# A four-layer vision block with a selective scan: the inputs of GpSimd's products moved to different 8-byte halves, and one more product in eight on GpSimd

## The chip, the core and the metric

The kernel runs on one core of a Trainium2 chip. The metric is the device time of one execution in microseconds (us). Before the change it is 22073.93 us, the median of three runs (22069.05 to 22075.93). The profile is of one such execution; its span from the first to the last instruction is 22054.7 us.

A core has engines that run at the same time, each with its own instruction queue, which it works through in order. TensorE (PE in the profile) multiplies matrices into PSUM, VectorE (DVE) and ScalarE (ACT) do elementwise work, GpSimd (POOL) does elementwise work [...], and SyncE (SP) issues most of the DMAs. They wait for each other through semaphores.

## What is computed

The input is 8 images of 56 x 56 positions with 192 channels, in float32. Four layers follow each other, each with a normalization ahead of it and a residual sum behind it: a gated layer with Toeplitz products, window attention, a 3 x 3 depthwise convolution, and a selective state-space layer. Only the last one is touched. Cut to what matters:

```python
def _selective_scan(u, delta, A, Bm, Cm, Dp, delta_bias):
    delta = jax.nn.softplus(delta + delta_bias[None, :, :, None])
    dA = jnp.exp(delta[:, :, :, None, :] * A[None, :, :, :, None])
    dBu = (delta * u)[:, :, :, None, :] * Bm[:, :, None, :, :]

    def comb(e1, e2):
        a1, b1 = e1
        a2, b2 = e2
        return (a1 * a2, a2 * b1 + b2)
    _, hs = jax.lax.associative_scan(comb, (dA, dBu), axis=-1)
    y = jnp.einsum('bkdnl,bknl->bkdl', hs, Cm)
    return y + Dp[None, :, :, None] * u
```

Per image there are 384 channels, 16 states per channel, 4 scan directions and 3136 positions. For each of them the state is h[t] = dA[t] * h[t-1] + dBu[t], and the output is the sum of h * C over the 16 states. Behind the scan come a layer normalization, a gate and a projection.

## The kernel before, in words

**Tiles of the scan.** An image's scan is cut into 28 chunks: 4 directions (`slot`) by 7 pieces of CH = 448 positions. Slots 0 and 2 run forward, slots 1 and 3 backward. The 384 channels are ND = 3 blocks of 128 partitions (`d`), the 16 states are NP = 8 groups of NG = 2 (`k`). One (chunk, d, k) is a *pair*: 2 states x 448 positions = 896 elements on 128 partitions. A chunk is 24 pairs, an image 672, the whole kernel 5376.

**What a pair does**, in the order of its steps (line numbers are those of the profile):

- `inject` (L1000, GpSimd): `ring[slot] = du * bm`, 896 elements. `du` is delta times x, 448 elements, read twice (once per state); `bm` is a row of B that a DMA has spread over the partitions. `ring` has 6 slots of 2 x 449 elements. Of the 449, one holds the state carried over from the chunk before (`initial`, L1007, ScalarE), at the front for a forward scan and at the back for a backward one.
- `decay` (L1017, ScalarE): two exponentials of delta, 449 elements each, into PSUM (`ps_a`, two buffers).
- `scan` (L1026, VectorE): one scan over 898 elements, from `ps_a` and the ring slot.
- `times_c` (L1032): `hc = h * cm`, 896 elements. `on_pool` (L995) says which engine takes it: GpSimd for k = 1, 4 and 6, else VectorE. [...]for its pairs the scan writes its result back into the ring slot; for VectorE's pairs it goes to `ps_a`. `hc` has four buffers.
- `keep_state` (L1039, ScalarE): the last state of the chunk is copied out of wherever the scan has put it.
- `add_up` (L1047, TensorE): two matmuls with the identity add the two states into `ps_y`. In float32 each is done in two passes, so the profile counts four. This frees the `hc` buffer.

Three times per chunk GpSimd also makes a `du` (`times_x`, L988, 448 elements, from `delta` and `xcd`).

**Where the tiles begin.** Each tile begins on a multiple of 32 bytes. A ring slot is 2 x 449 x 4 = 3592 bytes, which is 8 more than a multiple of 16, so even slots begin in the lower 8-byte half [...] and odd slots in the upper one; inside a slot, a forward pair begins 4 bytes on and its second state 1796 bytes behind the first. `delta2`, of which one buffer serves even chunks and the other odd ones, has rows of 450 x 4 = 1800 bytes, again 8 more than a multiple of 16, and its data begin 4 bytes into the row. `bm`, `cm`, `xcd` and `du` begin on a multiple of 16.

**The order of the work.** The order of all instructions is fixed when the program is built. The loop over pairs at L1197 writes out, for pair g: `inject(g+2)`, `times_c(g-1)` if it is GpSimd's, `keep_state(g-1)`, `decay(g+1)`, the scan of g, `times_c(g)` if it is VectorE's, the loads of B and C of the next chunk (`load_bc`, on SP's queue), then other work, then `add_up(g-2)`.

The other work comes from a planner (`Parts`, L1062). While image b is scanned, all earlier layers of image b+1 (`front`, L890: `gate`, `attention`, `conv2`, `inner`, `steps`) are put between the pairs in small pieces, and so is the end of image b's own output (`finish`, L897; layer normalization, gate and projection for one piece of 448 positions). The planner keeps a clock for each of four engines (P for GpSimd, A for ScalarE, D for VectorE, E for TensorE) and adds to it the cost in us that the code states for each step: 2.09 for an inject, 2.0 for a GpSimd `times_c`, 1.08 for a `du`, 2.02 for a scan, 1.09 for a VectorE `times_c`, 1.1 for `add_up`; the pieces of other work cost what `Meter` works out from their size. A piece is placed at pair g when its engines' clocks stay under limits that depend on the next scan (L1250); a piece that was refused gets 3 us of grace for each refusal. If something of image b+1 isn't ready when its scan needs it (L1205), the planner places the rest at once, with no pair between.

`finish` has two GpSimd products of 672 elements (L927, L934) on pieces that are carved one behind the other out of one tile, `slab_f`.

Image 0's earlier layers, and the first layer's products for all images, run ahead of the first scan. Image 7's scan has no next image beside it.

Of the kernel before, what the change touches and what calls it, by code (L numbers as in the profile page):

```python
# [15 lines left out]
F32 = mybir.dt.float32  # L16
# [11 lines left out]
CH = 448  # L28
# [6 lines left out]
TC = 24  # L35
NG = 2
NP = NS // NG
SLAB, SLAB_F = 10048, 2688


class Meter:
# [41 lines left out]
def model(ctx: ExitStack, tc: tile.TileContext, a: dict, out: bass.AP):  # L83
# [211 lines left out]
    with (  # L295
# [600 lines left out]

        def finish(b, j):  # L897

            yc, sq, rs, x3 = carve(slab_f, 128, (ND, CH), (ND, CH // 2), (CH // 2,), (2, CH // 2))
            x3 = x3[:CP]  # L900
            n = CH // 2

            def mean(p, src, n):
                for d in range(ND):
                    nc.tensor.matmul(p[:, :n], ones, src[:, d, :], start=d == 0, stop=d == ND - 1)  # L905

            y = ysum[:, :, j * CH : (j + 1) * CH]
            yield 0, 1
            p = bank()
            mean(p, y, CH)  # L910
            yield 1, 0
            nc.vector.tensor_sub(yc, y, p[:, :CH].unsqueeze(1).to_broadcast([128, ND, CH]))  # L912
            for u in range(2):
                yield 0, 0
                tok = slice(j * CH + u * n, j * CH + (u + 1) * n)
                yu = yc[:, :, u * n : (u + 1) * n]
                nc.scalar.activation(sq, yu, AF.Square)  # L917
                yield 0, 1
                p = bank()
                mean(p, sq, n)  # L920
                yield 1, 0
                nc.scalar.activation(rs, p[:, :n], AF.Ln, bias=eps5)  # L922
                nc.scalar.activation(rs, rs, AF.Exp, scale=-0.5)  # L923
                nc.sync.dma_start(out=sq, in_=z_d[b][:, :, tok])
                nc.sync.dma_start(out=x3, in_=blocks(x3_d[b])[:, :, tok])
                yield 0, 0
                nc.gpsimd.tensor_mul(yu, yu, rs.unsqueeze(1).to_broadcast([128, ND, n]))  # L927
                yield 0, 0
                for d in range(ND):
                    nc.scalar.activation(  # L930
                        yu[:, d, :], yu[:, d, :], AF.Identity, scale=ln_g[:, d : d + 1], bias=ln_b[:, d : d + 1]
                    )
                yield 0, 0
                nc.gpsimd.tensor_mul(yu, yu, sq)  # L934
                yield 0, 1
                p = bank()
                for m in range(2):
                    for d in range(ND):
                        nc.tensor.matmul(  # L939
                            p[:CP, m * n : (m + 1) * n],  # L940
                            w_out[:, d, m * CP : (m + 1) * CP],
                            yu[:, d, :],
                            start=d == 0,
                            stop=d == ND - 1,
                        )
                    yield 1, 0
                nc.vector.tensor_add(x3, x3, p[:CP, :CH].rearrange("p (m n) -> p m n", m=2))
                nc.sync.dma_start(out=blocks(out[b])[:, :, tok], in_=x3)
            yield 0, 0
# [34 lines left out]
            nc.sync.dma_start(out=delta[:, :, 1 : CH + 1], in_=dl_d[slot][b][:, :, j * CH : (j + 1) * CH])  # L984

        def times_x(i, d):
            du = dus[i, d] = sp.tile([128, 1, CH], F32, name="du", bufs=3)
            nc.gpsimd.tensor_mul(du[:, 0, :], deltas[i][:, d, 1 : CH + 1], xcs.pop((i, d)))  # L988

        def tokens(i):  # L990

            return (slice(0, CH), CH, 0) if chunks[i][1] % 2 else (slice(1, CH + 1), 0, CH)

        def on_pool(d, k):
            return k in (1, 4, 6)  # L995

        def inject(g):
            i, d, k = pairs[g]
            hs = hss[g] = ring[:, g % 6]
            nc.gpsimd.tensor_mul(hs[:, :, tokens(i)[0]], dus[i, d].to_broadcast([128, NG, CH]), bms[i, k])  # L1000

        def initial(g):

            i, d, k = pairs[g]
            at = NG * (NP * d + k)
            src = zero6 if i % NCH == 0 else states[i - 1].rearrange("p d n -> p (d n)")[:, at : at + 3 * NG]
            nc.scalar.copy(ring[:, g % 6 : g % 6 + 3, :, tokens(i)[1]], src.rearrange("p (q n) -> p q n", n=NG))  # L1007

        def decay(g):
            i, d, k = pairs[g]  # L1010
# [143 lines left out]
        sp = own.enter_context(tc.tile_pool(name="sc", bufs=2))  # L1154
        bcp = own.enter_context(tc.tile_pool(name="bc", bufs=NP))
        ysum = wp2.tile([128, ND, L], F32, name="ysum")
        ring = wp2.tile([128, 6, NG, CH + 1], F32, name="ring")
        delta2 = wp2.tile([128, 2, ND, CH + 2], F32, name="delta2")

        for u in range(2):  # L1160
            nc.gpsimd.memset(delta2[:, u, :, 0 : CH + 2 : CH + 1], 1e30)
# [3 lines left out]
        with tc.manual_schedule():  # L1165
# [11 lines left out]

            def feed(g):
                inject(g)
                fed[g] = run("P", 2.09, taken[g - 6] if g > 5 else 0.0)  # L1180

            def take(g):
                times_c(g)
                after = scanned[g], summed[g - 4] if g > 3 else 0.0
                taken[g] = run("P", 2.0, *after) if on_pool(*pairs[g][1:]) else run("D", 1.09, *after)

            def prepare(g):
                decay(g)
# [8 lines left out]
            for g, (i, d, k) in enumerate(pairs):  # L1197
# [13 lines left out]
                    xcs[i + 1, 2] = load_xc(i + 1, 2)  # L1211
                if more and (d, k) in ((1, 6), (1, 7), (2, 6)):
                    times_x(i + 1, k - 6 if d == 1 else 2)
                    run("P", 1.08)
                pi, pd, pk = pairs[g - 1]
                if g + ahead <= last:
                    feed(g + ahead)
# [145 lines left out]
```

## Time and profile before

| | |
|---|---|
| median of 3 runs | 22073.93 us |
| span of the profiled execution | 22054.7 us |
| PE busy | 18328.2 us (83%) |
| DVE busy | 16637.5 us (75%) |
| ACT busy | 12126.1 us (55%) |
| POOL busy | 16068.5 us (73%) |
| GpSimd's inject, L1000 | 5376 times, 2092 ns each |
| GpSimd's times_c, L1032 | 2016 times, 1958 ns each |
| GpSimd's du, L988 | 672 times, 1058 ns each |
| VectorE's times_c, L1032 | 3360 times, 1092 ns each |
| VectorE's scan, L1026 | 5376 times, 2.02 us each |
| PE, add_up, L1047 | 21504 passes, 591 ns each |

For the profiled execution the span is the only time of its own that is at hand; it is 19.2 us (0.1%) under the median of the runs.

Read such a table with care: a share of busy time is a mean over stages that have different limits. The first scan begins at 3441 us, image 7's at 19999 us. Between these two an image takes 2347 to 2393 us; image 7's scan, with no other image's work beside it, takes 2067 us to the end of the program. A group's mean can also hide several kinds of instruction: the 1958 ns of GpSimd's times_c is a mean over instructions that differ, as the prediction shows. Durations overlap a little on GpSimd: of two instructions that follow each other without a gap the second is reported to start before the first has ended.

### The profile page before, as it was taken

What the parts mean: (1) busy time and instruction counts of PE and PEld (TensorE: products, weight loads), DVE (VectorE), ACT (ScalarE), POOL (GpSimd) and SP (SyncE); (2) the same over time, 40 slices, a digit from 0 to 9 for tenths busy, and PEclk for the clock granted to TensorE, in tenths of its full rate; (3) what the DMA queues carried; (4) which work ended last, traced back from release to release, by engine and by line L of the source; (5) the groups of instructions that cost most, each with busy time, mean ns of one, the idle gap of its engine ahead of it and who ended that gap; (6) DMA issues with size and microseconds to landing.
All of it is one profiled execution on the core that took longest, in us unless ns stands there. A gap on an engine that the chain in (4) does not pass through costs nothing. (4 is left out here: it accounts for less than half of the span.)

```text
span 22054.7 us, 196675 instructions
## 1 busy us (share of the span) xinstructions
PE 18328.2 (83%) x58396; PEld 9752.3 (44%) x58396; DVE 16637.5 (75%) x13276; ACT 12126.1 (55%) x28153; POOL 16068.5 (73%) x8503
## 2 busy tenths in 40 slices
PE   7878977788887889888988888788988898887667
PEld 4845654334443444344443444344444444343333
DVE  2122117997799779987899789977998789977998
ACT  3125114655666465656665576656565666556554
POOL 0000007987889778987888788878898789878999
PEclk9588868999999989999999999898999999998888
DMA  3832575344644465345644464345534564445433
GB/s 88 239 99 49 177 186 165 122 130 162 185 138 125 145 194 152 121 129 180 185 124 128 159 196 137 123 147 189 159 117 131 176 186 125 126 151 184 129 127 110
DMA packets 2419588, 3249.95 MB, mean 147 GB/s; under 512 B 917598, under 2 KB 2361024, under 8 KB 2387554
## 3 DMA queue, kind: packets, MB, share of 16 engines
q1 hardware_dynamic: 2398292, 3121.12, 46.8%
q0 software_dynamic: 15520, 116.14, 1.4%
q8 instruction: 463, 7.59, 0.1%
q14 instruction: 609, 4.99, 0.1%
q10 hardware_dynamic: 4704, 0.12, 0.0%
HBM read 2661.35 MB, written 575.48 MB: 147 GB/s over the span
## 5 line engine op out<-in xcount | busy, mean ns | idle before, releaser
L1000 POOL TENSOR_TENSOR ring<-du,bm 128x896 f32<-128x896 f32 x5376 | 11104.3, 2092 | 17.3 <-DMA bm<-bc 10.1
L1047 PE MATMUL ps_y<-hc,ident_sb 128*128 128x448 f32 x21504 | 9809.0, 591 | 688.5 <-POOL hc L1032 620.9
L1026 DVE TENSOR_TENSOR_SCAN ps_a<-ps_a,ring 128x898 f32<-128x898 f32 x3360 | 6795.9, 2023 | 756.3 <-ACT ps_a L1017 295.2
L1017 ACT ACTIVATE ps_a<-delta,A_logs_sb 128x449 f32<-128x449 f32 x10752 | 6860.2, 638 | 327.8 <-DVE ring L1026 45.5
L1047 PEld LDWEIGHTS ps_y<-hc,ident_sb 128*128 128x128 f32 x21504 | 4281.7, 207 | 4745.4 <-issue 3574.5
L1032 POOL TENSOR_TENSOR hc<-ring,cm 128x896 f32<-128x896 f32 x2016 | 3947.5, 1958 | 2086.0 <-DVE ring L1026 991.9
L1032 DVE TENSOR_TENSOR hc<-ps_a,cm 128x896 f32<-128x896 f32 x3360 | 3668.4, 1092 | 1166.5 <-PE ps_y L1047 880.1
L1026 DVE TENSOR_TENSOR_SCAN ring<-ps_a,ring 128x898 f32<-128x898 f32 x2016 | 4063.3, 2016 | 276.6 <-ACT state L1039 121.0
L1039 ACT COPY state<-ps_a 128x2 f32<-128x2 f32 x3359 | 529.9, 158 | 4120.2 <-DVE hc L1032 4111.2
L278 DVE COPY tzx<-ps_tz 112x448 f32<-112x448 f32 x432 | 269.9, 625 | 1421.9 <-PE ps_tz L272 1289.2
L286 POOL DMA_DIRECT2D o<-tzx x192 | 97.4, 514 | 1686.4 <-DVE tzx L278 1552.5
L272 PE MATMUL ps_tz<-tzx,tm 112*112 112x112 f32 x4608 | 1031.7, 404 | 287.2 <-DMA tm<-ext 272.9
L272 PEld LDWEIGHTS ps_tz<-tzx,tm 112*112 112x112 f32 x4608 | 1028.1, 319 | 326.6 <-issue 320.5
L815 PE MATMUL ps_f<-slab 128*128 128x448 f32 x2646 | 1092.8, 549 | 55.3 <-DMA slab<-dg_d 48.1
L645 PE MATMUL ps_f<-ident_sb,slab 98*98 98x98 f32 x1344 | 335.8, 315 | 558.1 <-ACT slab L638 558.1
L747 PE MATMUL ps_f<-slab 96*96 96x448 f32 x1764 | 729.8, 549 | 42.5 <-DVE slab L734 42.5
L815 PEld LDWEIGHTS ps_f<-slab 128*128 128x128 f32 x2646 | 508.5, 193 | 555.8 <-issue 502.2
L77 PE MATMUL ps_f<-slab 96*96 96x448 f32 (+6 forms) x2306 | 737.8, 501 | 9.3 <-DMA slab<-x 4.1
L988 POOL TENSOR_TENSOR du<-delta,xcd 128x448 f32<-128x448 f32 x672 | 711.0, 1058 | 22.2 <-DMA slab<-in_x_dram 22.2
L1039 ACT COPY state<-ring 128x2 f32<-128x2 f32 x2016 | 378.7, 188 | 609.7 <-DVE ring L1026 581.0
L630 ACT ACTIVATE slab<-slab,mxs 98x98 f32<-98x98 f32 x1344 | 487.6, 364 | 357.8 <-DVE mxs L627 357.8
L482 PE MATMUL ps_f<-ident_sb,slab 112*96 112x112 f32 x4704 | 531.1, 267 | 138.3 <-DVE slab L490 95.0
(218 smaller groups left out, 16966.9 us busy)
## 6 DMA issues: line engine op xcount, KB each, us to landing
bm<-bc SPq DMA_DIRECT2D x1792, 448.0 KB
cm<-bc SPq DMA_DIRECT2D x1792, 448.0 KB
xcd<-xc SPq DMA_DIRECT2D x840, 224.0 KB
dl<-slab SPq DMA_DIRECT2D x224, 672.0 KB
delta<-dl SPq DMA_DIRECT2D x224, 672.0 KB
tzx<-qv SPq DMA_DIRECT2D x192, 588.0 KB
o<-tzx POOLq DMA_DIRECT2D x192, 588.0 KB, 14.2
slab<-x SPq DMA_DIRECT2D x224, 336.0 KB
```

What stands on the lines that cost most here:

```text
L77: return f(*args, **kw)
L272: nc.tensor.matmul(po[:, c, :], t[:, :, c2 + c], x[:, :, c1 + c2 + c], start=True, stop=True)
L482: nc.tensor.matmul(p[:CP, t * TT : (t + 1) * TT], ot[:, n % 2, i, t, c % 2 * CP : c % 2 * CP + CP], ident[:TT, :TT], start=i == 0, stop=i ...
L747: nc.tensor.matmul(p[:CP, :CH], dg[:, k, t, :], xp[:, u, k, dy : dy + 8, dx : dx + W], start=t == 0, stop=t == 8,)
L815: nc.tensor.matmul(p[:, :CH], dg[:, t, :], xp[:, 8 * j + dy : 8 * j + dy + 8, dx : dx + W], start=t == 0, stop=t == 8,)
L988: nc.gpsimd.tensor_mul(du[:, 0, :], deltas[i][:, d, 1 : CH + 1], xcs.pop((i, d)))
L1000: nc.gpsimd.tensor_mul(hs[:, :, tokens(i)[0]], dus[i, d].to_broadcast([128, NG, CH]), bms[i, k])
L1017: nc.scalar.activation(dA[:, n, :], deltas[i][:, d, at : at + CH + 1], AF.Exp, scale=negA[:, slot, d, c : c + 1])
L1026: nc.vector.tensor_tensor_scan(h, dA, hs, 0.0, ALU.mult, ALU.add)
L1032: (nc.gpsimd if on_pool(d, k) else nc.vector).tensor_mul(hc, h[:, :, tokens(i)[0]], cms[i, k])
L1039: nc.scalar.copy(states[i][:, d, NG * k : NG * k + NG], h[:, :, tokens(i)[2]])
L1047: nc.tensor.matmul(yps[i, d][:, :CH], ident, hcs[g][:, n, :], start=k + n == 0, stop=k + n == NP + NG - 2)
```

## The change

It has three parts.

1. **Where inputs begin.** Two elements (8 bytes, `HALF`) are put ahead of the data of `du`, `delta2` and, in `slab_f`, of the piece `sq` and what follows it. A ring slot becomes 900 elements (3600 bytes, a multiple of 16), and the 2 x 449 elements begin 1 element into it for a forward pair and 2 for a backward one, so that the positions themselves (without the carried state) begin 8 bytes [...] in either direction, and those of the second state 12 bytes. The other input (`bm`, `cm`, `xcd`, or the earlier piece of `slab_f`) begins at 0. So the two inputs of every GpSimd product begin in different 8-byte halves.
2. **Who multiplies by C.** `on_pool` gives GpSimd k = 0, 2, 4, 6 in place of k = 1, 4, 6: 12 of a chunk's 24 products in place of 9, or 2688 of 5376 in place of 2016.
3. **What the planner believes.** GpSimd's costs become 1.78 for an inject (2.09), 1.78 for a `times_c` (2.0) and 0.93 for a `du` (1.08).

```diff
-SLAB, SLAB_F = 10048, 2688
+HALF = 2
+SLAB, SLAB_F = 10048, 2688 + HALF
+SLOT = NG * (CH + 1) + HALF
...
-            yc, sq, rs, x3 = carve(slab_f, 128, (ND, CH), (ND, CH // 2), (CH // 2,), (2, CH // 2))
+            yc, _, sq, rs, x3 = carve(slab_f, 128, (ND, CH), (HALF,), (ND, CH // 2), (CH // 2,), (2, CH // 2))
...
-            du = dus[i, d] = sp.tile([128, 1, CH], F32, name="du", bufs=3)
+            du = dus[i, d] = sp.tile([128, 1, HALF + CH], F32, name="du", bufs=3)[:, :, HALF:]
...
         def on_pool(d, k):
-            return k in (1, 4, 6)
+            return k % 2 == 0
+
+        def in_ring(g, n):
+
+            at = 1 + chunks[pairs[g][0]][1] % 2
+            return ring[:, g % 6 : g % 6 + n, at : at + NG * (CH + 1)].rearrange("p q (n t) -> p q n t", n=NG)
 
         def inject(g):
             i, d, k = pairs[g]
-            hs = hss[g] = ring[:, g % 6]
+            hs = hss[g] = in_ring(g, 1)[:, 0]
...
-            nc.scalar.copy(ring[:, g % 6 : g % 6 + 3, :, tokens(i)[1]], src.rearrange("p (q n) -> p q n", n=NG))
+            nc.scalar.copy(in_ring(g, 3)[:, :, :, tokens(i)[1]], src.rearrange("p (q n) -> p q n", n=NG))
...
-        ring = wp2.tile([128, 6, NG, CH + 1], F32, name="ring")
-        delta2 = wp2.tile([128, 2, ND, CH + 2], F32, name="delta2")
+        ring = wp2.tile([128, 6, SLOT], F32, name="ring")
+        delta2 = wp2.tile([128, 2, ND, CH + 2 + HALF], F32, name="delta2")[:, :, :, HALF:]
...
-                fed[g] = run("P", 2.09, taken[g - 6] if g > 5 else 0.0)
+                fed[g] = run("P", 1.78, taken[g - 6] if g > 5 else 0.0)
...
-                taken[g] = run("P", 2.0, *after) if on_pool(*pairs[g][1:]) else run("D", 1.09, *after)
+                taken[g] = run("P", 1.78, *after) if on_pool(*pairs[g][1:]) else run("D", 1.09, *after)
...
-                    run("P", 1.08)
+                    run("P", 0.93)
```

## The prediction

> **What bounds the kernel now.** First the busy shares in 40 slices of the span (551 us each):
>
> ```profile
> PE   7878977788887889888988888788988898887667
> DVE  2122117997799779987899789977998789977998
> POOL 0000007987889778987888788878898789878999
> ```
>
> The scan runs from slice 7 on. No engine is full all the time: PE and DVE change places, and only in the last slices, where PE falls to 6, does POOL stand at 9. So I cut one middle image (scan from 10529 to 12877 us) by what the other work beside it is, and took the busy time of each stretch: gate, attention, conv2, inner, steps; the sixth row is a stretch of image 7, with nothing beside it.
>
> ```profile
> core 0: us, PE busy (x) PEld busy (x) DVE busy (x) ACT busy (x) POOL busy (x), PEclk, DMA share, GB/s
> 10659.00:11096.00 437.00, 409.94 (x1571) 226.80 (x1570) 404.30 (x310) 249.46 (x508) 379.36 (x199) 0.96 0.58 165
> 11096.00:11964.00 868.00, 681.30 (x2371) 333.91 (x2371) 817.18 (x691) 574.84 (x1673) 786.14 (x407) 0.92 0.41 125
> 11964.00:12145.00 181.00, 172.20 (x454) 79.00 (x453) 162.41 (x131) 71.91 (x167) 137.99 (x72) 0.98 0.41 124
> 12145.00:12703.00 558.00, 475.62 (x1293) 245.25 (x1293) 399.52 (x264) 309.41 (x629) 436.70 (x230) 0.92 0.51 165
> 12703.00:12991.00 288.00, 252.20 (x680) 116.00 (x676) 221.65 (x148) 240.12 (x429) 245.17 (x129) 0.92 0.62 209
> 20213.00:21551.00 1338.00, 914.33 (x1864) 403.12 (x1864) 1263.34 (x814) 680.80 (x1553) 1335.74 (x697) 0.87 0.40 130
> ```
>
> Gate and conv2 are TensorE's (94 and 95% busy), attention is VectorE's (94%; PE 78%), inner and steps are TensorE's in bursts (85 and 88%), and image 7 is GpSimd's (99.8%). TensorE's timeline in inner shows a burst: 4 passes of add_up, 6 of the convolution, and again, with no gap.
>
> ```profile
> 12242.36 1.67 PE L1047 MATMUL ps_y<-hc,ident_sb 128*128 128x448 f32 x4
> 12243.87 2.42 PE L815 MATMUL ps_f<-slab 128*128 128x448 f32 x6
> 12246.12 1.67 PE L1047 MATMUL ps_y<-hc,ident_sb 128*128 128x448 f32 x4
> ```
>
> From 12242.36 to 12246.12 is 3.76 us for a pair, where VectorE's own work per pair is 2.70 (2.02 + 5/8 x 1.09). There neither faster products nor fewer VectorE products help.
>
> **Does the half matter?** The kernel before answers it itself, since its ring slots begin in either half. GpSimd's timeline in a backward chunk of image 7:
>
> ```profile
> 20800.25 6.17 POOL L1000 TENSOR_TENSOR ring<-du,bm 128x896 f32<-128x896 f32 x3
> 20806.38 1.77 POOL L1032 TENSOR_TENSOR hc<-ring,cm 128x896 f32<-128x896 f32 x1
> 20808.11 6.17 POOL L1000 TENSOR_TENSOR ring<-du,bm 128x896 f32<-128x896 f32 x3
> 20814.24 2.07 POOL L1032 TENSOR_TENSOR hc<-ring,cm 128x896 f32<-128x896 f32 x1
> 20816.27 4.11 POOL L1000 TENSOR_TENSOR ring<-du,bm 128x896 f32<-128x896 f32 x2
> 20820.35 2.07 POOL L1032 TENSOR_TENSOR hc<-ring,cm 128x896 f32<-128x896 f32 x1
> 20822.38 6.17 POOL L1000 TENSOR_TENSOR ring<-du,bm 128x896 f32<-128x896 f32 x3
> 20828.50 1.78 POOL L1032 TENSOR_TENSOR hc<-ring,cm 128x896 f32<-128x896 f32 x1
> ```
>
> The counts between (3, 2, 3) tell that the products are k = 1, 4, 6, 1. k = 1 lies in an odd slot: both its states begin in the upper half (8 and 12 bytes), `cm` in the lower: 1.77 us. k = 4 and 6 lie in even slots (0 and 4 bytes), the half of `cm`: 2.07. Sorted over the whole trace, the 2016 products have means of 1777 ns (odd, backward), 2085 (even, backward), and 1935 and 1930 for forward ones, whose two states begin in different halves, so that one is with `cm` and one not. `du` splits likewise, by the row of `delta2`: 983 against 1133 ns. So in different halves 896 elements cost 0.31 us less, 448 elements 0.15. All injects, whose inputs both begin at 0, take 2087 ns (median), slot and direction make 4 ns at most: where the output begins doesn't matter.
>
> [...] In the trace the slope is (2085 - 1133) / 448 = 2.13 ns per element for one half, [...] but (1777 - 983) / 448 = 1.77 ns [...] for different halves[...]. [...] here an inject reported as 2.09 takes 2.04 of the queue (6.13 for three), a fast product 1.73, a slow one 2.03, a `du` 1.08 or 0.93. I use these.
>
> **The change, part by part.**
>
> *GpSimd per chunk.* Before: 24 injects x 2.04 + 9 products x 1.91 (mean of 1.73, 2.03 and 1.88 by their frequency) + 3 du x 1.0 = 69.2 us. Image 7 confirms it: 1338 us for 465 pairs (19.4 chunks) is 69.1. After: 24 x 1.73 + 12 x 1.73 + 3 x 0.93 = 65.1, or 4.1 less although three products are added. That an inject drops to 1.73 isn't in the trace (it reads `du` twice); bounds: 1.73, and 2.04 for no effect. I take 1.73, since at the same half it costs what a product costs (2087 against 2085), and `finish`'s two products, one with a repeated input, agree too (1613 and 1610 ns). Those save 0.23 us each, by the same slope; nobody waits there but in the last image.
>
> *VectorE per chunk.* 24 x 2.02 + 15 x 1.09 = 64.8 becomes 61.6: 3.3 less. Scans cost the same whichever tile they write (2016 and 2023 ns).
>
> *What moves.* k = 0 and 2 go to GpSimd, k = 1 goes to VectorE. A GpSimd product is issued one pair later, behind inject(g+2); the C load of the next chunk on SP's queue waits for it, so one load more per chunk is released up to 3 us later, ahead of a use a chunk away. keep_state reads the ring (188 ns, not 158): 20 us over the kernel on ScalarE, which has 40% free. add_up waits for GpSimd in 4 pairs of 8. In the last image TensorE already idles for it (415 us of 1338) at no cost; elsewhere four `hc` buffers cover it.
>
> *By stage, per image* (pairs per stage counted from the scans):
> - Attention, 272 pairs = 11.3 chunks, VectorE-bound: 11.3 x 3.3 = 37 us. GpSimd falls along (786 to about 740), so VectorE stays the bound.
> - Gate, 131 pairs: VectorE would give 18, but PE's 410 of 437 stays; 7 from the bubbles.
> - conv2, 48 pairs, PE and VectorE both near full: 3.
> - Inner, 142 pairs: bursts give nothing; between them pairs run at about GpSimd's 437/142 = 3.1 us and gain 0.15; with some 80 such pairs, 12.
> - Steps, 72 pairs, ScalarE and PE: 3.
>
> Sum 62, for 7 images 434. Image 7: 25 of its 28 chunks are GpSimd-bound, 25 x 4.1 = 103, with `finish` 105. VectorE follows at 61.6 to 65.1, no closer than before (64.8 to 69.2). What ran before 3441 us keeps its time. Total 539.
>
> *The planner.* Its pair gets shorter too, so it has less room per pair for the next image's layers. They begin later from image to image already: `steps` starts at pair 600 of 672 in the first scan, at 657 in the seventh, where the last chunk takes 127 us in place of some 90, since scans wait. A few pairs more per image will make that happen in several images; I take 50 us off: 489. Span 22054.7 - 489 = 21566, and with the 19 us by which the median exceeds the span, **21585 us**; this case's own range is 21450 to 21720. Chance 0.66.
>
> **Rivals.**
> - *The next image's layers fall behind.* If they stretch with the planner's pair (VectorE's 2.70 to 2.565, or 5%: some 30 pairs), they are late from the second image on. One late end costs 38 us (127 against 89), which was an overrun of about 10 pairs; 30 pairs cost about 68 us of bare TensorE work (2.26 each) plus waits, of which part comes back where TensorE is relieved: 45 net, five times: 225. 21810. For: the drift. Against: pieces mostly go one per pair, whatever the pair's length. 0.17.
> - *TensorE's stages gain as well*, because it waits less for products: a third of its idle 154 us per image outside attention, 26 more than I counted, 7 times, and no late ends: 21355. Against: it waited there for DMA, ScalarE and VectorE's small steps. 0.12.
> - *Slower: the repeated `du` hides the half.* Then the inject stays at 2.04, and GpSimd's chunk is 49.0 + 20.8 + 2.8 = 72.6, 3.4 more: image 7 loses 95, attention becomes GpSimd-bound and gains nothing, inner loses some 5 per image: 22190. It decides from an inject of 1.90 on, where the chunk is back at 69.2. 0.05.
>
> **Range and chances.** 21380 to 21850 leaves out the slower rival, the lower half of the gain in TensorE's stages and the worst of the late ends, about 2 in 10. A measurement here can tell 0.2% (44 us) from no change. Faster by more: 0.92; within: 0.03; slower: 0.05.
>
> **What would show it.** Injects and products all at 1.77 to 1.79 us, `du` at 0.98; 2688 products each; image 7's chunks at 65 to 66 us with GpSimd still near 100%; attention at about 830 us with VectorE near 94%; gate and conv2 almost unchanged. An inject above 1.9, chunks beyond 120 us at the ends of images 1 to 5, or attention with both VectorE and GpSimd under 90% would prove me wrong.

## The result, and the profile after

The change takes the median from 22074.93 us (4 runs, 22069.05 to 22098.8) to **21828.74 us** (4 runs, 21800.17 to 21848.46): 246 us less, a ratio of 0.9884 (95% interval 0.987 to 0.9898). The profiled execution spans 21798.4 us, 256 less than before. That is inside the range, and half of the 489 us that I had forecast.

The busy shares of the kernel after, in 40 slices (545 us each), for the three engines that were shown of before:

```profile
PE   7978977888888989888888889888988888887777
DVE  2122117996799768986799769976898589976998
POOL 0000006887789778977788768976898678877998
```

The last slices still read PE 7, POOL 9, DVE 9: image 7 remains GpSimd's. Next, groups of the page after: line, engine, operation, tiles and count, then busy time and mean ns of one, then the engine's idle time ahead of the group and what ended most of it.

```profile
L1007 POOL TENSOR_TENSOR ring<-du,bm 128x896 f32<-128x896 f32 x5376 | 9447.8, 1771 | 1983.9 <-ACT ring L1014 1937.8
L1039 POOL TENSOR_TENSOR hc<-ring,cm 128x896 f32<-128x896 f32 x2688 | 4758.0, 1770 | 860.9 <-DVE ring L1033 349.3
L1039 DVE TENSOR_TENSOR hc<-ps_a,cm 128x896 f32<-128x896 f32 x2688 | 2935.0, 1092 | 974.5 <-PE ps_y L1054 753.3
L990 POOL TENSOR_TENSOR du<-delta,xcd 128x448 f32<-128x448 f32 x672 | 658.6, 980 | 23.6 <-DMA xcd<-xc 23.6
```

The durations are what the change is meant to give: inject 1771 ns (2092 before), GpSimd's `times_c` 1770 (1958), `du` 980 (1058), 2688 products each. The surprise stands at the end of the first line: inject waited **1938 us** for ScalarE's L1014. That is `initial`, the copy of the carried states into the ring (L1007 before). Before, inject waited 17 us in all.

The same stages as in the prediction, for the same image (gate, attention, conv2, inner, steps; the sixth row is a stretch of image 7), as busy time of each engine in each stretch after the change:

```profile
core 0: us, PE busy (x) PEld busy (x) DVE busy (x) ACT busy (x) POOL busy (x), PEclk, DMA share, GB/s
10634.00:11064.00 430.00, 405.99 (x1578) 224.17 (x1576) 389.73 (x296) 249.86 (x512) 360.09 (x215) 0.98 0.58 160
11064.00:11892.00 828.00, 683.53 (x2375) 334.67 (x2375) 780.43 (x658) 575.06 (x1676) 742.01 (x445) 0.89 0.43 131
11892.00:12077.00 185.00, 175.62 (x458) 80.75 (x457) 156.45 (x128) 73.53 (x172) 133.51 (x80) 0.97 0.41 127
12077.00:12660.00 583.00, 488.09 (x1343) 259.36 (x1341) 355.22 (x233) 305.13 (x614) 386.04 (x235) 0.92 0.48 154
12660.00:12991.00 331.00, 274.24 (x666) 118.91 (x666) 233.75 (x150) 252.09 (x448) 248.29 (x150) 0.83 0.63 209
20030.00:21262.00 1232.00, 887.37 (x1790) 382.08 (x1790) 1149.26 (x723) 653.94 (x1489) 1205.41 (x722) 0.87 0.42 138
```

Attention went from 868 to 828 us with VectorE at 94% in both. Inner became longer, 583 against 558, although VectorE and GpSimd have less to do in it (355 against 400 us, 386 against 437). Image 7's GpSimd is at 97.8% where it was at 99.8%.

Two things about these rows have to be known. The stretches, here, in the prediction and for e12 below, were counted from the profiler's own zero, which lies 11.3 us ahead of the first instruction, while the view counts from that instruction; so each begins and ends 11 us after its stage. The same holds for the scan starts given ahead (3441 and 19999 us are 3430 and 19988 on the clock of the views; 10529 and 12877 are 10518 and 12866). Both kernels are shifted alike, and no busy share above moves by more than about three points. And the prediction's row for steps stops 36 us before the next gate begins: the stage took 324 us there, so its 288 must not be compared with the 331 here.

Taken over all images from the traces (each stage from the first matmul of its main work to that of the next; mean of 7 images, of 6 for steps), in us; these durations don't depend on where the clock starts:

| kernel | gate | attention | conv2 | inner | steps | sum | image 7 |
|---|---|---|---|---|---|---|---|
| before | 439.4 | 872.5 | 185.5 | 564.9 | 339.6 | 2401.9 | 2066.7 |
| after | 433.0 | 828.6 | 189.4 | 584.2 | 345.8 | 2381.0 | 1994.2 |
| change | -6.4 | -43.9 | +3.9 | +19.3 | +6.2 | -20.9 | -72.5 |
| forecast | -7 | -37 | -3 | -12 | -3 | -62 | -105 |

The forecast had 50 us of lateness besides. So attention gave more than I said, more than half of it was given back in the stages behind it, and image 7 gave two thirds. Another 26 us of the trace's 256 lie ahead of the first scan (3430 to 3404 us); the other runs' profiles have it between 3372 and 3423, so I take it for scatter.

### The profile page after: what moved, and what is told of

Same layout as the page of the kernel before. It is cut to its first block, busy times and chain, and to the rows that moved or that the text cites. A ratio compares the mean times of both kernels' runs of the same rounds, so it can differ in the third digit from the quotient of the medians.

```text
span 21798.4 us, 194536 instructions
## 1 busy us (share of the span) xinstructions
PE 18274.4 (84%) x58396; PEld 9706.4 (45%) x58396; DVE 15858.5 (73%) x12604; ACT 12098.2 (56%) x28153; POOL 15084.9 (69%) x9175
## 5 line engine op out<-in xcount | busy, mean ns | idle before, releaser
L1007 POOL TENSOR_TENSOR ring<-du,bm 128x896 f32<-128x896 f32 x5376 | 9447.8, 1771 | 1983.9 <-ACT ring L1014 1937.8
L1033 DVE TENSOR_TENSOR_SCAN ps_a<-ps_a,ring 128x898 f32<-128x898 f32 x2688 | 5429.0, 2020 | 1062.5 <-ACT ring L1014 555.0
L1033 DVE TENSOR_TENSOR_SCAN ring<-ps_a,ring 128x898 f32<-128x898 f32 x2688 | 5423.0, 2017 | 420.4 <-ACT state L1046 177.3
L1039 POOL TENSOR_TENSOR hc<-ring,cm 128x896 f32<-128x896 f32 x2688 | 4758.0, 1770 | 860.9 <-DVE ring L1033 349.3
L1039 DVE TENSOR_TENSOR hc<-ps_a,cm 128x896 f32<-128x896 f32 x2688 | 2935.0, 1092 | 974.5 <-PE ps_y L1054 753.3
L1046 ACT COPY state<-ps_a 128x2 f32<-128x2 f32 x2687 | 425.3, 158 | 3254.0 <-DVE hc L1039 3250.0
L1046 ACT COPY state<-ring 128x2 f32<-128x2 f32 x2688 | 504.9, 188 | 791.3 <-DVE ring L1033 778.4
L990 POOL TENSOR_TENSOR du<-delta,xcd 128x448 f32<-128x448 f32 x672 | 658.6, 980 | 23.6 <-DMA xcd<-xc 23.6
L647 PEld LDWEIGHTS ps_f<-ident_sb,slab 98*98 98x98 f32 x1344 | 203.9, 158 | 1033.7 <-ACT slab L640 814.6
L227 PE MATMUL ps_qv<-wqv,xn 96*128 96x384 f32 (+1 forms) x1200 | 527.0, 522 | 128.2 <-DVE xn L146 67.5
```

Source lines behind the costliest of these rows:

```text
L647: nc.tensor.transpose(p[:PT_, e * PT_ : (e + 1) * PT_], S[:, 3 * g + e, :], ident[:PT_, :PT_])
L1033: nc.vector.tensor_tensor_scan(h, dA, hs, 0.0, ALU.mult, ALU.add)
L1039: (nc.gpsimd if on_pool(d, k) else nc.vector).tensor_mul(hc, h[:, :, tokens(i)[0]], cms[i, k])
L1046: nc.scalar.copy(states[i][:, d, NG * k : NG * k + NG], h[:, :, tokens(i)[2]])
```

## The experiments

All ratios are to the kernel before, on the same chip. The diffs are against the kernel after unless another is named; lines in the `profile` fences follow each kernel's own numbering. Twelve kernels ran.

### 1. The halves alone, and the order alone

**e1** keeps the new tiles and takes back the two other parts, so that the order of the work is that of before.

```diff
-            return k % 2 == 0
+            return k in (1, 4, 6)
...
-                fed[g] = run("P", 1.78, taken[g - 6] if g > 5 else 0.0)
+                fed[g] = run("P", 2.09, taken[g - 6] if g > 5 else 0.0)
...
-                taken[g] = run("P", 1.78, *after) if on_pool(*pairs[g][1:]) else run("D", 1.09, *after)
+                taken[g] = run("P", 2.0, *after) if on_pool(*pairs[g][1:]) else run("D", 1.09, *after)
...
-                    run("P", 0.93)
+                    run("P", 1.08)
```

> The new starting halves alone: k = 1, 4, 6 stay on GpSimd and the planner keeps its old costs, so that every instruction stands where it stood before. If the halves act on GpSimd alone, its products all take 1.77 us, its chunk falls from 69.2 to 24 x 1.73 + 9 x 1.73 + 2.8 = 60 us, and image 7 becomes VectorE-bound at about 65.5 us a chunk in place of 69 (25 x 3.5 = 88 us). Attention, VectorE-bound, keeps its 76 us. Theory (the next image's layers came late and cost the rest of the forecast): 21930, with no chunk of over 130 us. Rival (TensorE's work sets images 0 to 6 whatever the planner does): image 7's gain alone, 21985.

Measured: 22145.26 us (7 runs), ratio 1.0031 (1.002 to 1.0042). **Slower**, with every GpSimd product at 1772 to 1773 ns. No theory of mine allowed that, and so I looked for what else the tiles had changed. **e3** has the planner's new costs with the old choice of k.

```diff
-            return k % 2 == 0
+            return k in (1, 4, 6)
```

> The new halves and the planner's new costs, with GpSimd keeping k = 1, 4, 6. By the order of the program the next image's layers fall behind slowly and come late only in the last two scans, with no 47 matmuls in one go. Theory: VectorE keeps its 64.8 us a chunk, so attention stays at 76; near the kernel with the halves alone, 21900 to 21960. Rival (lower planner costs alone bring the late ends): chunk 28 of several images over 130 us, and 22000 or more.

Measured: 22109.75 us (20 runs), 1.0019 (1.0013 to 1.0026): the planner's costs aren't the reason. **e2** has the new tiles and the new choice of k with the planner's old costs (the last three edits of e1).

> The new halves and the new share of GpSimd (k even), with the planner's old costs (2.09, 2.0, 1.08). Compared with the changed kernel only the placement of other work differs. By the order of the program, the steps of the next image begin at pairs 597, 612, 625, 639, 649, 655, 655 of 672, not at 656 from the fourth image on with 47 convolution matmuls in one go. Theory (late ends took about 70 us in each of four images): chunk 28 of images 3 to 6 goes from 163 us to 90 to 100, and the time from 21829 to about 21600. Rival (the same TensorE work only moves into other chunks): within 40 us of 21829.

Measured: 21871.73 us (4 runs), 0.9902 (0.9887 to 0.9916). Images are numbered from 0. The last chunks of 163 us that images 3 to 6 have after the change, of which more below, are gone in its trace (95 to 117 us), and nothing was gained. **e4** is the reverse, edited from the kernel before: the old tiles, with the new k and the new costs, so the order of the kernel after with the slow products.

```diff
-            return k in (1, 4, 6)
+            return k % 2 == 0
...
-                fed[g] = run("P", 2.09, taken[g - 6] if g > 5 else 0.0)
+                fed[g] = run("P", 1.78, taken[g - 6] if g > 5 else 0.0)
...
-                taken[g] = run("P", 2.0, *after) if on_pool(*pairs[g][1:]) else run("D", 1.09, *after)
+                taken[g] = run("P", 1.78, *after) if on_pool(*pairs[g][1:]) else run("D", 1.09, *after)
...
-                    run("P", 1.08)
+                    run("P", 0.93)
```

> The program order of the changed kernel, to the instruction, with the old starting halves: GpSimd's injects take 2.09 us and its products 1.77 to 2.09. Its chunk is 24 x 2.04 + 12 x 1.91 + 3 = 75 us. Theory: image 7's chunks go to 75 us (25 x 6 = 150 us more than before), attention becomes GpSimd-bound at about 76 and gains nothing, and the late ends cost their 290 us: about 22450. Rival (the halves are worth little outside image 7): under 22150.

Measured: 22404.43 us (4 runs), 1.0145 (1.0128 to 1.0162), as expected: without the halves three more products per chunk only load GpSimd. Image 7 takes 2221 us there, with GpSimd busy for 1498 us of a stretch of 1500.

### 2. A wait that the diff doesn't show

The idle time of the carry copy tells what is wrong. First the group in the kernel before:

```profile
L1007 ACT COPY ring<-state 128x6 f32<-128x6 f32 x1536 | 283.4, 185 | 0.0
```

In the kernel after:

```profile
L1014 ACT COPY ring<-state 128x6 f32<-128x6 f32 x1536 | 291.8, 190 | 503.5 <-POOL ring L1007 502.9
```

The copy now waits for inject, and inject for the copy. The waits of e1, on GpSimd's and then on ScalarE's side (engine, tile and line, what it waited for: us in total, times, longest):

```profile
POOL ring L1007 <- ACT ring L1014: 2457.7, 1144, 15.7
...
ACT ring L1014 <- POOL ring L1007: 453.0, 198, 145.7
```

In the built program each of the 1536 copies carries a wait for GpSimd; none of those 1536 did before. The order of each engine's instructions is the same in e1 and before, so only the tiles can have brought the wait. Within a chunk the bytes don't overlap: inject writes the 448 positions of a row and the copy the one element beside them. But `ring` was a tile of [6, 2, 449], whose row and element were separate indices; now it is [6, 900], with rows of 449 laid into it by an offset, and the copy has steps of 900 and 449. I take it that the program's builder holds the two for overlapping; how it decides isn't shown, only that the wait comes with these tiles and goes with e5's. What follows is a lockstep: GpSimd may not go on to the injects of the pairs that the copy serves until ScalarE has come to it, behind all that stands in ScalarE's queue.

**e5** has the halves without that: a uniform tile [6, 2, 452] whose positions begin at element 2 in either direction, the carried state beside them. The price is a scan of 902 elements (2031 ns, not 2023) and exponentials of 452 (641 ns, not 638). k and the costs are those of before.

```diff
-SLOT = NG * (CH + 1) + HALF
+ROW = CH + 2 * HALF
...
-            return (slice(0, CH), CH, 0) if chunks[i][1] % 2 else (slice(1, CH + 1), 0, CH)
+            at = slice(HALF, HALF + CH)
+            return (at, HALF + CH, HALF) if chunks[i][1] % 2 else (at, HALF - 1, HALF + CH - 1)
...
-            hs = hss[g] = in_ring(g, 1)[:, 0]
+            hs = hss[g] = ring[:, g % 6]
...
-            nc.scalar.copy(in_ring(g, 3)[:, :, :, tokens(i)[1]], src.rearrange("p (q n) -> p q n", n=NG))
+            nc.scalar.copy(ring[:, g % 6 : g % 6 + 3, :, tokens(i)[1]], src.rearrange("p (q n) -> p q n", n=NG))
...
-        ring = wp2.tile([128, 6, SLOT], F32, name="ring")
+        ring = wp2.tile([128, 6, NG, ROW], F32, name="ring")
```

> The halves alone, as in the kernel with only the new layout, but without the wait that came with it: GpSimd's inject no longer waits for ScalarE's copy of the carried states, nor that copy for the inject. The ring is a tile of 6 x 2 rows of 452 elements, its positions from element 2 in either direction, so that the carried states of three slots lie in one column (one step of 452) and never in an inject's columns; the scan runs over 902 elements, not 898, and an exponential over 452, not 449. GpSimd's k is 1, 4, 6 and the planner's costs are old: the order is that of the kernel before. Theory (the wait tied GpSimd to ScalarE's queue, 2458 us of GpSimd's idle time): inner and steps back to 565 and 340 us, image 7 at about 66 us a chunk; 21950. Rival (faster products themselves disturb the order, by reaching PSUM and hc buffers at other times): within 40 of 22145.

Measured: 21990.39 us (4 runs), 0.9947 (0.9932 to 0.9962). The same two groups in e5:

```profile
L1003 POOL TENSOR_TENSOR ring<-du,bm 128x896 f32<-128x896 f32 x5376 | 9406.9, 1774 | 46.1 <-DMA bm<-bc 28.7 <-ACT ps_a L1019 11.2 <-ACT state L1041 5.1
...
L1010 ACT COPY ring<-state 128x6 f32<-128x6 f32 x1536 | 283.4, 185 | 0.0
```

The copy's idle time is 0.0 again and inject's 46 us; in the built program none of the 1536 copies carries the wait. With order and product speed alike, e1 and e5 differ by 0.84% of the kernel (1.0031 against 0.9947): steps is 359.5 us per image in e1 and 340.9 in e5, inner 568.2 and 563.3, image 7 2023.8 and 1994.8. That is about what e5's theory said (21950 us, inner 565, steps 340). **e8** looks at the wait from the other side: it is the kernel before with rows laid into flat slots, at offsets that leave both inputs of each inject and of each GpSimd `times_c` in the same half.

```diff
+SLOT = NG * (CH + 1) + 6
...
+        def in_ring(g, n):
+            at = 3 + chunks[pairs[g][0]][1] % 2
+            return ring[:, g % 6 : g % 6 + n, at : at + NG * (CH + 1)].rearrange("p q (n t) -> p q n t", n=NG)
...
-            hs = hss[g] = ring[:, g % 6]
+            hs = hss[g] = in_ring(g, 1)[:, 0]
...
-            nc.scalar.copy(ring[:, g % 6 : g % 6 + 3, :, tokens(i)[1]], src.rearrange("p (q n) -> p q n", n=NG))
+            nc.scalar.copy(in_ring(g, 3)[:, :, :, tokens(i)[1]], src.rearrange("p (q n) -> p q n", n=NG))
...
-        ring = wp2.tile([128, 6, NG, CH + 1], F32, name="ring")
+        ring = wp2.tile([128, 6, SLOT], F32, name="ring")
```

> The kernel before with the wait alone: ring slots of 904 elements, in which both states of a pair begin in the lower half in either direction, so that GpSimd's products stay slow (all 2.09 us, where 7 of 18 states were fast in the kernel before: 1 us a chunk more), and the copy of the carried states and the injects wait for each other as in the changed kernel. The order of the work is that of the kernel before. Theory: image 7 at 70 us a chunk (+27 us), steps 20 us and inner and gate some 5 us longer per image: 22250 to 22350. Rival (the wait is harmless as long as GpSimd is slow): 22080 to 22120.

Measured: 22502.44 us (4 runs), 1.018 (1.0165 to 1.0196), more than expected. Two of its groups:

```profile
L1005 POOL TENSOR_TENSOR ring<-du,bm 128x896 f32<-128x896 f32 x5376 | 11135.3, 2090 | 1476.9 <-ACT ring L1012 1354.7 <-ACT state L1044 89.6 <-DVE ysum L1064 10.5
...
L1037 POOL TENSOR_TENSOR hc<-ring,cm 128x896 f32<-128x896 f32 x2016 | 4193.8, 2080 | 735.3 <-PE ps_y L1052 239.9 <-issue 225.9 <-DVE ring L1031 215.3
```

The wait is there, but the kernel isn't a clean measure of it: the second line shows 2080 ns where the kernel before has 1958, since its odd slots have no fast products any more. That is 246 us of GpSimd's time, or 1.1% of the kernel, if all of it counted; in image 7, where it does, it is 28 x 9 x 0.122 = 31 of the 87 us by which the image is longer than before. So with products of 2.09 us the wait alone costs between 0.7 and 1.7%; with those of 1.77 us 0.84%. For the halves e8 is a control: its tile is flat like that of the change, and with their inputs in the same half inject takes 2090 ns and `times_c` 2080. So it is the half that makes them fast, and not the new shape of the tile.

### 3. The whole change without the wait

**e6** is the whole change on e5's tile. Against e5:

```diff
-            return k in (1, 4, 6)
+            return k % 2 == 0
...
-                fed[g] = run("P", 2.09, taken[g - 6] if g > 5 else 0.0)
+                fed[g] = run("P", 1.78, taken[g - 6] if g > 5 else 0.0)
```

with the planner's other two costs likewise as in the change.

> The whole change (halves, k even, new costs, the same order of work), without the wait between the inject and the copy of the carried states, by the same layout with rows of 452 elements. Theory: steps, conv2 and inner each get shorter by what the wait took (20, 4 and 5 us per image in the kernels so far), image 7 to about 65.3 us a chunk: 21640. Rival (late ends, not the wait, took the rest): 21800 to 21830.

Measured: 21747.45 us (4 runs), 0.9832 (0.9815 to 0.9848): 0.52% better than the change itself, with about 0.2% of uncertainty in that difference. It lies between the theory and the rival. The stages did not get shorter as the theory had it (steps 345.1 us, conv2 188.0 and inner 584.0, against 345.8, 189.4 and 584.2 with the wait); image 7 did. What GpSimd waits for in place of the copy, in e6:

```profile
POOL hc L1034 <- DVE ring L1028: 1183.9, 636, 47.5
...
POOL hc L1034 <- PE ps_y L1049: 564.7, 270, 47.7
```

It now waits for the scan (1184 us) and for free `hc` buffers (565 us), so over the whole program it isn't the bound. In image 7, where it is the bound, the wait for the copy can be seen singly. GpSimd's timeline after the change (start, us, line, tiles; in brackets the idle time before and who ended it):

```profile
20396.65 1.78 POOL L1007 TENSOR_TENSOR ring<-du,bm 128x896 f32<-128x896 f32 x1
20398.73 1.77 POOL L1007 TENSOR_TENSOR ring<-du,bm 128x896 f32<-128x896 f32 x1 [0.31 <-ACT ring L1014]
20400.46 1.77 POOL L1039 TENSOR_TENSOR hc<-ring,cm 128x896 f32<-128x896 f32 x1
20402.19 3.50 POOL L1007 TENSOR_TENSOR ring<-du,bm 128x896 f32<-128x896 f32 x2
...
20412.56 1.76 POOL L1007 TENSOR_TENSOR ring<-du,bm 128x896 f32<-128x896 f32 x1
20414.65 1.77 POOL L1007 TENSOR_TENSOR ring<-du,bm 128x896 f32<-128x896 f32 x1 [0.32 <-ACT ring L1014]
```

A fast product is followed after 1.73 us (20400.46 to 20402.19), but 20396.65 to 20398.73 is 2.08: 0.35 lost, and again 16 us later, three times in a chunk. It makes a steady chunk 66.1 us long, against 65.1 in e6, which is the prediction's figure, and the chunks that share GpSimd with `finish` 74 to 76 against 70 to 71. Image 7 takes 1994.2 us with the wait and 1959.6 without: 35 us. In the profiled executions images 0 to 6 end alike (image 7's scan begins at 19804 and 19802 us), though the medians differ by more than these 35; what the wait costs between the two is not resolved. **e7** has e6's tile with the planner's old costs.

> As the previous one, with the planner's old costs: no late ends with 47 matmuls in one go. With the wait in place, old costs gave 21872 against 21829, so the late ends cost nothing net. Theory: the same difference holds without the wait, 21640 to 21700. Rival (the wait had hidden what the late ends cost): 21550 or less.

Measured: 21790.62 us (4 runs), 0.986 (0.9845 to 0.9876). That is outside both forecasts. The new costs are worth little: 0.28% here, 0.18% with the wait (e2), about the size of the intervals.

### 4. Do the late ends cost the rest?

In images 3 to 6 the next image's layers aren't done when the scan needs them, and the last chunk takes 163 us where it took 89 to 92 before (127 in the seventh scan). VectorE's timeline in such a chunk, after the change:

```profile
12618.62 2.02 DVE L1033 TENSOR_TENSOR_SCAN ring<-ps_a,ring 128x898 f32<-128x898 f32 x1
12667.81 2.04 DVE L1033 TENSOR_TENSOR_SCAN ps_a<-ps_a,ring 128x898 f32<-128x898 f32 x1 [47.17 <-ACT ring L1014]
```

No scan runs for 47 us. In the order of the program, pair 656 of 672 is where it happens: 47 matmuls stand there between two scans, 15 of inner's convolution and 12 of steps from the next image, 18 of `finish` and 2 of add_up (not 47 of the convolution, as the expectation of e2 had it). But TensorE doesn't work through this gap. For 30.9 of the 47 us it waits for the DMA that brings inner's result to steps, and for the most of that time ScalarE is still finishing inner: the late end is a chain through ScalarE, DMA and TensorE. `steps` begins at pairs 603, 629, 655 and from then on 656; in the order of before it moves from 597 to 656 over seven images. **e9** lets the planner's TensorE clock run 3 us further ahead in the kernel after, **e10** does the same in e6.

```diff
-                parts.step({"A": max(n2, fed[g + 2]) - 0.7, "E": n1 + 5.0, "D": 0.2})
+                parts.step({"A": max(n2, fed[g + 2]) - 0.7, "E": n1 + 8.0, "D": 0.2})
```

> The changed kernel, carry wait included, with one number of the planner raised: TensorE's clock may run 8 us past the next scan's start, not 5. By the order of the program the next image's layers then start their steps at pairs 599 to 649 and nothing is placed in one go; attention keeps its 272 pairs. Theory (the late ends cost time): chunk 28 of images 3 to 6 from 163 to about 95 us, some of it given back in inner, 100 to 200 us in all: 21650 to 21730. Rival (TensorE's work in inner and steps costs the same wherever it stands, as old costs suggested): within 40 us of 21829.

> The change without the carry wait (rows of 452) and with the same limit of 8 us. Theory: both losses are gone, 21560 to 21620. Rival: 21750, as without the wait alone.

Measured: e9 21909.78 us, 0.9916 (0.9901 to 0.9931), e10 21728.44 us, 0.9833 (0.9818 to 0.9848), 4 runs each. The late ends are gone in both (last chunks of 95 to 108 and 89 to 98 us before image 7), and e10 takes the time of e6, as its rival had it, while e9 is slower than the change, which neither of its forecasts allowed. With e2 and e7 that makes four kernels without the long ends, and none is faster than its partner by more than the intervals. **The theory that late ends eat the gain falls.** Why taking out a gap in which TensorE waits 31 us gains nothing is not shown. **e11** lets ScalarE's clock run 0.7 us further in e6.

```diff
-                parts.step({"A": max(n2, fed[g + 2]) - 0.7, "E": n1 + 5.0, "D": 0.2})
+                parts.step({"A": max(n2, fed[g + 2]) - 0.0, "E": n1 + 5.0, "D": 0.2})
```

> The change without the carry wait, with the other limit moved: ScalarE's clock may run to the start of the scan after next, not 0.7 us less. By the order of the program, attention shrinks from 272 pairs to 258, the next image's layers are done up to 90 pairs ahead of need, and nothing is placed in one go. Theory (late ends cost time; ScalarE has room): 21550 to 21620. Rival (the 0.7 us keep ScalarE's exponentials on time for the scans, so VectorE waits for them instead): 21750 to 21850.

Measured: 21840.98 us (4 runs), 0.9891 (0.9875 to 0.9908): slower than e6, and what its rival said, in number and in kind: over the program VectorE waits 866 us for ScalarE's exponentials, where it waits 455 in e6. Attention is spread over 257 pairs there, not 272, and takes the same time, 831 us; 30 us of it VectorE now waits for exponentials, and next to none in e6. So the moved limit costs what the fewer pairs save, and e11 doesn't tell whether attention would get shorter if the exponentials came in time.

### 5. What bounds the stage that became longer?

**e12** takes TensorE's work out of inner alone. It is the kernel after with the last three of the nine taps of inner's 3x3 filter left out, in all images, while the planner still counts them, so VectorE's and GpSimd's orders stay as they are.

```diff
+                        if t > 5:
+                            if nc is meter:
+                                meter.log.append(("E", 0.04 + 1.25e-3 * CH))
+                        else:
+                            nc.tensor.matmul(
...
-                            stop=t == 8,
+                                stop=t == 5,
```

> The changed kernel with three of the nine taps of the 3 x 3 convolution in inner left out (the last row of the filter, in all images), while the planner still counts them: VectorE's and GpSimd's orders are the same to the instruction, and TensorE has 126 passes of 0.376 us, or 47 us, less to do per image. Theory (TensorE sets the time of inner, which is why the changed kernel gained nothing there): inner falls by 35 to 47 us per image, the whole by 280 to 370, to about 21500. Rival (the chain of scan, products and copies sets it, with TensorE's bursts only filling gaps): inner falls by less than 15 us, the whole stays above 21700.

Measured: 21485.54 us (4 runs), 0.9734 (0.9718 to 0.9751). Its inner stage (the same image; columns as in the stages above):

```profile
11943.00:12476.00 533.00, 442.86 (x1216) 236.16 (x1215) 354.00 (x233) 306.29 (x613) 385.93 (x235) 0.91 0.51 168
```

VectorE has 354 us of work in it and GpSimd 386, as in the kernel after (355 and 386); TensorE has 45 us less, and the stage is 50 us shorter. As a mean of the seven images, inner falls from 584.2 to 543.2 us, 41 for some 47 us of matmuls taken out (126 passes, at the 0.376 us that each of the ten passes of a 3.76 us burst takes). They stood in 21 bursts. If TensorE set the pace in the burst pairs alone, each could at best fall from 3.76 us to VectorE's own 2.57 (2.02 + 1/2 x 1.09), which is 25 us in all, an estimate from the durations above. So TensorE sets the pace of the convolution's part of inner, in the pairs between as well. The rest of inner (the products ahead of each convolution) e12 doesn't test.

## Why the prediction was right in kind and wrong in size

**Right: the halves.** All three kinds of GpSimd product have the duration I read out of the kernel before, the inject too, on which the slower rival rested (1771 ns; it would have decided from 1900 on).

**Right: attention and gate.** Attention gave 43.9 us per image for 37, gate 6.4 for 7. VectorE stayed the fullest engine of attention.

**Wrong: "between them pairs run at about GpSimd's 3.1 us".** This is the failed step of the stage sum. I booked 12 us for inner, 3 for conv2 and 3 for steps on the ground that GpSimd is close to full between TensorE's bursts. e5 has the faster products, the order of before and no added wait: inner 563.3 us (564.9 before), conv2 184.2 (185.5), steps 340.9 (339.6). So faster products give nothing in these stages. For inner the kernel before shows why: what GpSimd and VectorE wait for there is TensorE, which hasn't freed the `hc` buffer. Waits in its stretch (total us, times, longest):

```profile
DVE hc L1032 <- PE ps_y L1047: 86.9, 53, 7.1
...
POOL hc L1032 <- PE ps_y L1047: 45.0, 15, 7.8
```

TensorE for its part waits for GpSimd's `times_c` in 9 of an inner's 565 us and for a product of `finish` in 11 (mean of seven images). So GpSimd, full as it looked, was the one that waited; and e12 confirms it where the convolution stands. For conv2 and steps no run takes TensorE's work out, and there the cause stays open. In TensorE's timeline of inner the period of a burst is what it was, 3.76 us (12182.40 to 12186.16):

```profile
12182.40 1.67 PE L1054 MATMUL ps_y<-hc,ident_sb 128*128 128x448 f32 x4
12183.91 2.42 PE L817 MATMUL ps_f<-slab 128*128 128x448 f32 x6
12186.16 1.67 PE L1054 MATMUL ps_y<-hc,ident_sb 128*128 128x448 f32 x4
```

TensorE's granted clock is hardly the reason in inner: 0.93 before and 0.92 after, with a pass of add_up at 558 ns in both (means; over the program 0.891 and 0.888, and 591 ns in both). In steps it fell from 0.87 to 0.84 (mean of six images), which may be part of that stage's 6 us. In place of -18 these three stages take +29 us per image; with the 50 us that I had allowed for lateness, that is -76 forecast and +206 measured over seven images, 282 of a miss. Part of it is work that only changed place: inner holds 1339 matmul passes where it held 1310, steps 708 where it held 752 (means). Images 0 to 2 are 35 to 58 us shorter than before, but each leaves some 26 pairs' worth of the next image's layers over, while images 3 to 6 take 2358 to 2366 us, against 2349 to 2393 before. **Once the ends come late, an image gains about nothing.** Over images 0 to 6 the mean gain is 23 us an image; in the kernels without the long ends it is 31 (e10) and 14 (e9), each from one profiled execution. My reading is that TensorE has the same 18.3 ms to do in either kernel (busy 18328 us before, 18274 after), and that what attention no longer covers has to be done elsewhere; that is argued, not shown. How the 25 us of inner and steps together split into late ends, waits and shifted work is not settled.

**Missed: the wait.** I went through what the change removes, adds and moves, and never asked whether the new shape of `ring` alters what waits for what. It costs 35 us of image 7 (1994 us, where I had forecast 1962 and e6 measured 1960) and 0.52% of the whole by e6's median, of which I can place only these 35.

**Lateness.** The forecast gave it 50 us in all, on the argument that pieces go one per pair whatever the pair's length. That failed: the layers did stretch, by some 26 pairs an image, and the last chunks of images 3 to 5 went to 163 us, which the prediction had named, from 120 us on, as a sign of being wrong. The rival had the stretch right (30 pairs) and with 45 us net for each late end said 21810, near what was measured. But the late ends don't eat the gain: e2, e7, e9 and e10 take the long ones away, and the time stays or grows. A near number with a cost that wasn't there.

**The account.** Against the forecast of -489: attention 49 us better, gate 4 worse, conv2, inner and steps with the lateness 282 worse, image 7 32 worse, 26 us found ahead of the first scan: 243 short, where the trace lacks 233 (steps is a mean of six images and counts seven times here).

**Best version.** e6 and e10, the change on a uniform tile, are the fastest that do all the work (0.983 of before).

## What to carry to other kernels

When a tile gets another shape or is indexed in another way, list for each pair of engines that touch it which waits the built program has before and after; instructions with disjoint bytes can still be made to wait for each other, as 1536 copies and the injects were here. Book the saving of an engine only in those stages where it is the bound, and check a claim about a mixed stage by taking out work of the engine that you believe sets it. Work that is filled in beside a loop and comes late leaves a gap that is easy to see, but the gap isn't by itself time that can be won: here four kernels closed the long ones, and none was faster by more than the intervals.

## What the hardware showed

- The two halves are worth only as much as GpSimd's time is: in e5 they take 13% off its busy time (16069 to 13940 us) and 0.53% off the kernel, in the trace all of it in image 7 and ahead of the first scan. The interval of an instruction in the queue follows: from start to start, a product reported as 1.77 us takes 1.73 (20400.46 to 20402.19 after the change), as it did for k = 1 before.
- The starts count modulo 16 bytes. In the kernel before, slots 0 to 5 of the ring begin 0, 8, 16, 24, 0 and 8 bytes past a multiple of 32, and in backward chunks GpSimd's `times_c` takes 2085, 2085 and 2086 ns from slots 0, 2 and 4, and 1777, 1778 and 1777 ns from slots 1, 3 and 5 (means over the trace). What in GpSimd makes the half matter isn't shown.
- An input that is read twice makes no difference to this: inject reads `du` for both of its states and takes 1771 ns, `times_c` 1770.
